# Later slots for the last normalising passes of the V slice, and a new order of work in the first group of a pre-normalised graph attention layer

## The chip, the cores and the metric

The kernel runs on one core of one Trainium2 chip, as a single launch. The metric is the device time of that launch in microseconds (us), from the start of the program to its end. A profiled execution also gives a span, from the first to the last recorded instruction.

## The reference

128 graphs of 128 nodes with 768 features each are normalised, rectified and sent through 12-headed attention (64 features a head) that is masked and biased by an adjacency matrix. All data are float32.

```
h = jnp.maximum(_layernorm(x, axis=-1), 0.0)
q, k, v = split(h @ Wq + bq), split(h @ Wk + bk), split(h @ Wv + bv)
scores = einsum('bhqd,bhkd->bhqk', q, k) / sqrt(64) + beta * adj
scores = where(adj > 0, scores, -9e15)
out = x + merge(softmax(scores) @ v)
```

## The kernel before, in words

**Groups and slices.** The 128 graphs are taken in 32 groups of four (G = 0 to 31). A group goes through three slices of matrix products: "qk0" (queries and keys of heads 0 to 5), "v" (all values) and "qk1" (queries and keys of heads 6 to 11). The scores, the softmax and the weighting of one group's heads are woven between the products of the slices that follow.

**Products.** A slice is a 3x3 block product. For groups 1 to 31 it is done with 15 block products (`PRODUCTS`) in place of 18. In qk0 and v each of them is done once more with seven small products on 128 columns (`product_z`, L482), for which the weights must first be turned into sums: `prepare` (L245) makes these once, during group 0, and stores them in DRAM (tensors `kept_qk` and `kept_v`). From there `load_T` (L292) brings them through a ring of five buffers (tag "T"), 448 KB for each product. The making of the sums uses the same ring of five, so a new sum waits until an older one has been stored.

Group 0 has no such sums yet. `plain_slice` (L761) gives it plain products: for each row half r (graphs 0-1, then graphs 2-3) and each output column block j it fills one PSUM bank with three steps k. Its matmuls are on L779. The q and k results are read out by ScalarE (L800), those of V by VectorE (L792).

**Slots.** A slot is one product (15 in a slice, `run`, L743), or one step k of `plain_slice` (18 in a slice). The dictionary `todo` lists what else is issued in a slot: after its matmuls and ahead of its read-out, or, with "post", behind the read-out. `then(at, f, ...)` enters it. From the V slice of group 0 on (`tc.manual_schedule()`, L978) each engine's queue follows the order of the code. Ahead of that line, so in qk0 of group 0, a planner with its own costs puts each engine's instructions in order, and `tc.issue_after(i)` is the means to force one instruction behind another on its engine.

**Openings.** The 15 products add up in four chains a, b, c, d of two PSUM banks each, and the bank's running sum is read out after each product. The first time that an output block is used, its tile is opened: ScalarE copies most of the banks (L509 and L511 for V, L514 to L517 for q and k) after VectorE has done a part of them (L508, L510). Later uses are VectorE additions (L521, L522). In `ZORDER` the products of slots 0, 1, 2, 3, 5 and 6 open a tile; those of slot 4 and of slots 7 to 14 only add. Slot 6 is product 5 of chain a, and the next product of chain a is product 10 in slot 8, which writes to the same banks.

**Normalising.** `norm` (L396) is four ScalarE passes for one graph (L400, in place on `x`). It needs the graph's rstd and shift. For groups 1 and 2 these come from `stats` (L316, VectorE), `moments_1` (L326: two small matmuls on L332, then VectorE) and `moments_2` (L342: matmuls on L346, VectorE, GpSimd); for group 0 in the same way for graphs 2-3 (`half`, L885) and by rows for graphs 0-1. `to_hT` (L402, VectorE, L406) then transposes a third of two graphs into a tile A00 to A12, where the first digit is the row half. Behind group 1 the V slice of group G normalises group G+1: graphs 0 and 1 in the posts of slots 0 to 3, graph 2 in slot 4 and graph 3 in slot 5 (L1040), and it transposes A01, A00, A02 and A11 in slots 5, 6, 7 and 9.

**Transfers.** All large transfers are issued by SyncE, in the order of its queue. `load_x` (L158) brings two graphs of x with four transfers into one of two buffers; `raw_qk` (L202) loads weight columns, eight transfers for the whole third slice (tile `wqk1`); `add_raw` (L922) loads a group's adjacency. A store of `kept_qk` or `kept_v` (L256) waits for GpSimd (L253, L254), which for most raw blocks waits for copies on ScalarE (L276).

Of the kernel before, what the change touches and what calls it, by code (L numbers as in the profile page):

```python
# [10 lines left out]
F32 = mybir.dt.float32  # L11
# [103 lines left out]
def direct(ctx, tc, x, adj, wq, bq, wk, bk, wv, bv, beta, out, bad):  # L115
# [645 lines left out]
    def plain_slice(G, sl, todo, rows=(0, 1)):  # L761

        n = 0
        for r in rows:
            for j in range(3):
                bank = take()
                p = bank.rearrange("p (i w) -> p i w", i=2)

                parts = (slice(0, N), slice(N, H2)) if sl == "qk0" and r == j == 0 else (slice(0, H2),)
                for at, k in [(at, k) for at in parts for k in range(3)]:  # L770
                    a, b = A[G, f"A{r}{k}"], wt[sl, f"B{k}{j}"]
                    for i in range(2):
                        for c in range(2):
                            lhs, rhs = b[:, c, i], a[:, c, at]
                            if sl == "v":
                                lhs, rhs = a[:, c, i * N:(i + 1) * N], b[:, c].rearrange("p i n -> p (i n)")
                            for q in range(0, P, HD) if sl == "qk1" else (slice(0, P),):
                                q = slice(q, q + HD) if sl == "qk1" else q
                                last = nc.tensor.matmul(p[q, i, at], lhs[:, q], rhs, start=(k == 0 and i == 0 and c == 0),  # L779
                                                        stop=(c == 1), skip_group_check=True)  # L780
                            turn()
# [188 lines left out]
    for r in range(2):  # L970
        then(5, load_x, 1, r)
    then(8, lambda: raw_qk(1, const.tile([P, NC * VH * 2], F32, name="wqk1"), ((0, 3),)))
    for n in range(5, 18):
# [7 lines left out]
    for g in range(GRP):  # L981
        then(2 * g, stats, 1, g)
        then(12 + g, norm, 1, g)
    then(8, lambda: mom.extend(moments_1(1, 0, GRP * NB)))
    then(10, lambda: moments_2(1, 0, GRP * NB, *mom))
    for n in range(18):
# [15 lines left out]
    for n in range(RING):  # L1002
        then(12 + n, load_T)
    then(13, add_raw, 1)
    plain_slice(0, "qk1", todo, (1, 0))

    for G in range(1, NG):
# [11 lines left out]
        if G == 1:  # L1019
            bias(1, 0, 2, 3, 5)  # L1020
            for r in range(2):
                then(r, load_x, 2, r)
            for g in range(GRP):
                then(5 + 2 * g, stats, 2, g)
            then(6, add_raw, 2)
# [9 lines left out]
        if more:  # L1035
# [3 lines left out]
            for g in range(2, GRP):  # L1039
                then(2 + g, norm, G + 1, g)  # L1040
            for name, at in (("A01", 5), ("A00", 6), ("A02", 7), ("A11", 9)):
                then(at, to_hT, G + 1, int(name[1]), int(name[2]))
# [177 lines left out]
```

## Time and profile before

| what | value |
|---|---|
| median of 3 runs | 2828.64 us (2823.12 to 2829.03) |
| the profiled execution | 2829.12 us |
| its span | 2827.0 us |
| TensorE matmuls busy | 2753.4 us, 97% of the span |
| granted TensorE clock, mean | 0.993 |

TensorE's own time is the first thing to look at, then what it waits for: the kernel's views list, for each engine, whom it waited for, how long in total, how often, and the longest wait. A timeline row gives start, duration, engine, line, operation, tiles and shape of merged instructions, and in brackets the idle time ahead of them and what ended it. A float32 matmul appears as two records. An engine's row in a window tells its busy time and count there, then the granted clock (PEclk), the busy share of the DMA engines and GB/s. Times that are given as places (such as "at 80.00") are us from the start of the span.

### The profile page before, as it was taken

The page shows a single profiled execution, that of the slowest core. Times are in us where ns is not written, and L with a number is a line of the kernel's source. Part 1 is how long each engine was busy: PE and PEld are TensorE (multiplying, and loading weights), DVE is VectorE, ACT ScalarE, POOL GpSimd, SP SyncE. Part 2 cuts the span into 40 slices and gives each one's busy share as a digit, 9 for nine tenths or more (in the row PEclk, how much of TensorE's full clock was granted, in tenths as well). Part 3 has the DMA queues.
Part 4 walks back from the last instruction along what each step waited for, and adds up shares of the span by engine and source line. Part 5 has one row for each costly group of instructions (what it writes and reads, how often), then busy time and mean ns, then how long its engine had stood idle before and what let it go on. Part 6 is the DMA issues. An engine that isn't in the chain of part 4 may idle for free.

```text
span 2827.0 us, 113416 instructions
## 1 busy us (share of the span) xinstructions
PE 2753.4 (97%) x46433; PEld 2391.0 (85%) x46433; DVE 2187.4 (77%) x4826; ACT 1357.7 (48%) x3999; POOL 2293.8 (81%) x4054
## 2 busy tenths in 40 slices
PE   8989999999999999999999999999999999999998
PEld 7678888888888888888888888888888888888887
DVE  3888777787777788787787787877777887877865
ACT  2345454555444554445553545554545544455533
POOL 2678988888888889888889888888888898888893
PEclk8999999999999999999999999999999999999999
DMA  9587778788778778778877788878787877788854
GB/s 220 188 253 223 235 225 248 253 244 236 230 225 260 250 237 234 229 233 260 249 231 233 227 244 257 246 231 234 222 260 250 235 236 231 231 259 249 234 182 130
DMA packets 526216, 660.87 MB, mean 234 GB/s; under 512 B 105460, under 2 KB 401664, under 8 KB 525696
## 3 DMA queue, kind: packets, MB, share of 16 engines
q1 hardware_dynamic: 525368, 653.20, 77.4%
q8 instruction: 368, 6.03, 0.9%
q14 instruction: 152, 1.25, 0.1%
q10 hardware_dynamic: 328, 0.40, 0.1%
HBM read 589.26 MB, written 64.21 MB: 231 GB/s over the span
## 4 chain that ended last, share of the span: by engine, by line


## 5 line engine op out<-in xcount | busy, mean ns | idle before, releaser
L630 ACT ACTIVATE o<-bank,sm 128x64 f32<-128x64 f32 x1524 | 355.0, 316 | 657.2 <-DVE sm L624 468.4
L495 PE MATMUL bank<-spbuf,T_qk 128*64 128x128 f32 x7440 | 658.7, 273 | 0.9 <-POOL qk L543 0.5
L495 PE MATMUL bank<-T_v,spbuf 128*64 128x128 f32 x7440 | 646.1, 273 | 0.1
L646 PEld LDWEIGHTS bank<-v,e 128*64 128x64 f32 x6048 | 412.3, 137 | 110.6 <-ACT o L630 0.2
L495 PEld LDWEIGHTS bank<-T_v,spbuf 128*64 128x64 f32 x7440 | 458.8, 137 | 0.4 <-ACT o L630 0.4
L495 PEld LDWEIGHTS bank<-spbuf,T_qk 128*64 128x64 f32 x7440 | 439.2, 137 | 1.4 <-POOL qk L543 0.8
L495 PE MATMUL bank<-T_v,S 128*64 128x128 f32 x4092 | 403.3, 274 | 36.0 <-ACT v L509 35.4
L646 PE MATMUL bank<-v,e 128*64 128x65 f32 x6048 | 433.8, 221 | 0.1
L581 ACT ACTIVATE qk<-bank,bqk 128x256 f32<-128x256 f32 x372 | 156.8, 475 | 550.8 <-PE bank L571 439.4
L495 PE MATMUL bank<-S,T_qk 128*64 128x128 f32 x4092 | 401.5, 274 | 4.2 <-DMA T_qk<-kept_qk 3.0
L571 PE MATMUL bank<-S,wqk 128*64 128x256 f32 x2976 | 389.2, 380 | 0.0
L613 DVE SCALAR_TENSOR_TENSOR e<-bank,biasT 128x512 f32<-128x512 f32 x378 | 240.5, 685 | 89.4 <-PE bank L609 89.3
L571 PE MATMUL bank<-S,qk_T 128*64 128x256 f32 x2480 | 305.3, 379 | 0.0
L495 PEld LDWEIGHTS bank<-T_v,S 128*64 128x64 f32 x4092 | 258.7, 137 | 49.4 <-ACT v L509 42.6
L521 DVE TENSOR_TENSOR v<-v,bank 128x512 f32<-128x512 f32 x310 | 211.8, 683 | 110.0 <-PE bank L495 96.6
L656 POOL TENSOR_TENSOR xo<-xo,o 128x512 f32<-128x512 f32 x189 | 242.0, 1280 | 58.9 <-ACT o L630 58.9
L551 POOL TENSOR_TENSOR v<-v 128x128 f32<-128x128 f32 x186 | 86.1, 463 | 223.6 <-ACT x L400 198.4
L521 DVE TENSOR_TENSOR qk<-qk,bank 128x512 f32<-128x512 f32 x310 | 210.7, 680 | 70.7 <-PE bank L495 34.8
L495 PEld LDWEIGHTS bank<-S,T_qk 128*64 128x64 f32 x4092 | 247.8, 137 | 14.8 <-issue 5.2
L587 DVE TENSOR_TENSOR qk<-qk,bank 128x512 f32<-128x512 f32 (+1 forms) x311 | 208.3, 670 | 43.4 <-PE bank L571 32.1
L616 ACT ACTIVATE e<-e 128x512 f32<-128x512 f32 x378 | 231.0, 632 | 21.8 <-DVE e L613 20.1
L418 POOL TENSOR_TENSOR spbuf<-S 128x128 f32<-128x128 f32 x341 | 182.9, 537 | 44.1 <-DVE S L411 44.1
(164 smaller groups left out, 5902.4 us busy)
## 6 DMA issues: line engine op xcount, KB each, us to landing
T_qk<-kept_qk SPq DMA_DIRECT2D x465, 448.0 KB, 5.0
T_v<-kept_v SPq DMA_DIRECT2D x465, 448.0 KB, 4.8
x<-in_x_dram SPq DMA_DIRECT2D x254, 192.0 KB, 4.7
xo<-in_x_dram SPq DMA_DIRECT2D x189, 256.0 KB, 5.1
out_dram<-xo SPq DMA_DIRECT2D x189, 256.0 KB, 5.0
half<-in_x_dram SPq DMA_DIRECT2D x232, 192.0 KB, 3.8
adj<-in_adj_dram SPq DMA_DIRECT2D x128, 64.0 KB, 2.5
kept_qk<-prep_qk SPq DMA_DIRECT2D x15, 448.0 KB, 3.9
```

The lines of the kernel that those rows point to most:

```text
L418: e.tensor_tensor(t[:, 0], a[:, 0, N:H2], a[:, 1, N:H2], ALU.add)
L495: nc.tensor.matmul(p[z // 4][q:q + HD, z % 4, :], lhs[:, q:q + HD], rhs, start=(first and z % 4 == 0), stop=True, skip_group_check=True)
L521: nc.vector.tensor_tensor(t[:, 0:4], t[:, 0:4], p[0], op)
L551: e.tensor_tensor(v[:, 0:2, 0:HD], heads(0), heads(3), ALU.add)
L571: nc.tensor.matmul(p[q:q + HD, i, :], lhs[:, q:q + HD], rhs, start=(first and i == 0 and c == 0), stop=(c == 1), skip_group_check=True)
L581: opened[0] = nc.scalar.activation(t[:, i, :], p[:, i, :], AF.Identity, bias=bqk[:, i, oc:oc + 1], scale=float(sign))
L587: added[G] = nc.vector.tensor_tensor(t[:, :, cols], t[:, :, cols], p[:, :, cols], ALU.add if sign > 0 else ALU.subtract)
L613: taken[0] = nc.vector.scalar_tensor_tensor(e, ps[oc, i].rearrange("p (g n) -> p g n", g=GRP), SCORE_CAP * ISCALE, biasT[G], op0=ALU.min, ...
L616: nc.scalar.activation(e, e, AF.Exp, scale=1.0 / ISCALE)
L630: nc.scalar.activation(o[:, b], pa[:, b, 0:HD], AF.Copy, scale=t[:, 1, b:b + 1])
L646: nc.tensor.matmul(pa[q:q + HD, 2 * g + i, :], es[G, oc, i][:, 2 * r + g, q:q + HD], vt[G, "v", r, h // 4][:, 4 * g + h % 4, :], start=Tru ...
L656: nc.gpsimd.tensor_add(t, t, o.rearrange("p a (b j) d -> p (a b) (j d)", j=2))
```

## The change

There are five edits.

1. In `plain_slice`, for the slice qk0 of group 0, every matmul of the second row half (graphs 2-3) is forced behind the last matmul of the first row half.
2. The loading of the third slice's weights (`raw_qk(1, ...)`, eight transfers) goes from slot 8 of that slice, in the planner's part, to slot 4 of the V slice of group 0, in the part that is ordered by the code.
3. In the V slice of group 0 the moments of group 1 go from slots 8 and 10 to 9 and 11, and its normalising passes from slots 12 to 15 to 13 to 16.
4. In the qk1 slice of group 0 the adjacency of group 1 is loaded in slot 11 and no longer in slot 13, and graphs 2-3 of group 2 in slot 16 (before: slot 1 of the next slice). Graphs 0-1 of group 2 go from slot 0 to slot 1 of that next slice, and its statistics take graphs 2, 3, 0, 1 in this order.
5. In the V slices of groups 1 to 30, the passes of graphs 2 and 3 of the next group go from slots 4 and 5 to slots 8 and 9, and the transpose A11 from slot 9 to slot 11.

```diff
     def plain_slice(G, sl, todo, rows=(0, 1)):
         n = 0
+        row0 = None
         for r in rows:
             for j in range(3):
+                row0 = last if (r, j) == (1, 0) and sl == "qk0" else row0
...
-                                last = nc.tensor.matmul(p[q, i, at], lhs[:, q], rhs, start=(k == 0 and i == 0 and c == 0),
-                                                        stop=(c == 1), skip_group_check=True)
+                                with ExitStack() as behind:
+                                    if sl == "qk0" and r == 1:
+                                        behind.enter_context(tc.issue_after(row0.ins))
+                                    last = nc.tensor.matmul(p[q, i, at], lhs[:, q], rhs, start=(k == 0 and i == 0 and c == 0),
+                                                            stop=(c == 1), skip_group_check=True)
...
-    then(8, lambda: raw_qk(1, const.tile([P, NC * VH * 2], F32, name="wqk1"), ((0, 3),)))
     for n in range(5, 18):
         then(n, after, step, 1 + n % 2)
     plain_slice(0, "qk0", todo)
...
     for g in range(GRP):
         then(2 * g, stats, 1, g)
-        then(12 + g, norm, 1, g)
-    then(8, lambda: mom.extend(moments_1(1, 0, GRP * NB)))
-    then(10, lambda: moments_2(1, 0, GRP * NB, *mom))
+        then(13 + g, norm, 1, g)
+    then(4, lambda: raw_qk(1, const.tile([P, NC * VH * 2], F32, name="wqk1"), ((0, 3),)))
+    then(9, lambda: mom.extend(moments_1(1, 0, GRP * NB)))
+    then(11, lambda: moments_2(1, 0, GRP * NB, *mom))
...
-    then(13, add_raw, 1)
+    then(11, add_raw, 1)
+    then(16, load_x, 2, 1)
     plain_slice(0, "qk1", todo, (1, 0))
...
-            for r in range(2):
-                then(r, load_x, 2, r)
+            then(1, load_x, 2, 0)
             for g in range(GRP):
-                then(5 + 2 * g, stats, 2, g)
+                then(5 + 2 * g, stats, 2, (g + 2) % GRP)
...
             for g in range(2, GRP):
-                then(2 + g, norm, G + 1, g)
-            for name, at in (("A01", 5), ("A00", 6), ("A02", 7), ("A11", 9)):
+                then(6 + g, norm, G + 1, g)
+            for name, at in (("A01", 5), ("A00", 6), ("A02", 7), ("A11", 11)):
                 then(at, to_hT, G + 1, int(name[1]), int(name[2]))
```

## The prediction

> **What bounds the kernel now.** I read the engines' busy times first, then the list of waits of TensorE (PE), then the timeline around each of its waits.
>
> ```profile
> PE 2753.4 (97%) x46433; PEld 2391.0 (85%) x46433; DVE 2187.4 (77%) x4826; ACT 1357.7 (48%) x3999; POOL 2293.8 (81%) x4054
> ```
> ```profile
> PE bank L495 <- ACT v L509: 35.4, 30, 1.2
> PE bank L779 <- DVE A L406: 6.9, 1, 6.9
> PE bank L332 <- DVE st L321: 6.7, 1, 6.7
> ```
>
> PE is busy 97% of the span, so a microsecond is only to be had where PE stands still or runs slowly. The list has one wait that comes back (30 times 1.2 us, for the opening copy L509 of V) and two long single ones. The first belongs to edit 5, the other two to edits 1 to 3, all in group 0. Here is one V slice, of group 4: ScalarE (ACT), PE, VectorE (DVE), then the slice's window.
>
> ```profile
> 449.91 4.49 ACT L400 ACTIVATE x<-x,block 128x192 f32<-128x192 f32 x10
> 454.30 0.47 ACT L509 ACTIVATE v<-bank 128x384 f32<-128x384 f32 x1
> ...
> 454.94 0.48 ACT L509 ACTIVATE v<-bank 128x384 f32<-128x384 f32 x1
> ...
> 468.16 0.47 ACT L581 ACTIVATE qk<-bank,bqk 128x256 f32<-128x256 f32 x1 [12.48 <-PE bank L571]
> ```
> ```profile
> 455.47 0.44 PE L495 MATMUL bank<-T_v,S 128*64 128x128 f32 x4 [1.18 <-ACT v L509]
> ```
> ```profile
> 452.80 0.29 DVE L510 TENSOR_TENSOR v<-bv_b,bank 128x128 f32<-128x128 f32 x1
> ...
> 457.81 0.70 DVE L406 STREAM_TRANSPOSE A<-x 128x512 f32<-128x512 f32 x1
> ```
> ```profile
> 440.00:468.00 28.00, 26.82 (x508) 24.97 (x505) 21.03 (x43) 14.83 (x35) 19.79 (x37) 1.00 0.85 273
> ```
>
> Ten passes in a row hold ACT from 449.91 to 454.40: two from the post of slot 3 and the eight of graphs 2 and 3. The openings of slots 5 and 6 stand behind them. The second copies its first bank out until 455.42, and PE, which wants that bank for product 10 in slot 8, starts at 455.47. The window's 28.00 less 26.82 is that same 1.18: PE has no other hole in this slice, and its clock stays at 1.00.
>
> **Edit 5, the V slices of groups 1 to 30.** No work is added or removed. Without the eight passes (8 x 0.45 = 3.6 us) ACT is free at about 450.9. DVE has finished its part of the second opening at 453.09 (L510), so ACT's two copies, 0.48 and about 0.4, end near 453.8. PE would start slot 8 at 455.47 - 1.18 = 454.29. So 0.5 us stay in hand, and the wait goes. The moved passes now run from 453.8 to 457.4, where ACT had nothing until 468.16; that 12.48 is their cover. A11 in slot 11 is issued two products later than at 457.81, so it finds graph 3 ready. DVE, next in line, had done slot 7's sum before PE came to slot 9. I see no other wait that comes in its place, except in group 1:
>
> ```profile
> 203.87 0.44 PE L495 MATMUL bank<-T_v,A 128*64 128x128 f32 x4 [2.48 <-DVE v L521]
> ```
>
> There DVE, loaded with weight sums and masks, holds PE later in the same slice, and PE would only arrive 1.18 us earlier at that wait. So the term is 29 x 1.18 = **34.2 us** (35.4 if group 1 gains too).
>
> **Edit 1, the order in qk0 of group 0.** PE's timeline there:
>
> ```profile
> 20.39 0.29 PE L332 MATMUL bank<-st,mean 128*64 128x16 f32 x4
> 21.66 0.29 PE L346 MATMUL bank<-dev,mean 128*64 128x16 f32 x4 [0.97 <-DVE dev L339]
> 28.85 28.89 PE L779 MATMUL bank<-A,spbuf 128*128 128x256 f32 x120 [6.90 <-DVE A L406]
> 57.58 10.52 PE L779 MATMUL bank<-spbuf,A 128*128 128x256 f32 x48
> ...
> 80.00 0.43 PE L332 MATMUL bank<-st,mean 128*64 128x32 f32 x4 [6.71 <-DVE st L321]
> 80.36 6.29 PE L779 MATMUL bank<-spbuf,A 128*128 128x256 f32 x16
> ```
> ```profile
> 28.00:34.00 6.00, 5.15 (x12) 4.17 (x13) 5.92 (x12) 0.64 (x4) 2.28 (x3) 0.50 1.03 203
> ```
> ```profile
> 80.00:85.00 5.00, 5.00 (x15) 4.04 (x16) 4.79 (x14) 1.40 (x6) 2.33 (x3) 0.50 0.57 223
> ```
>
> At 20.68 PE has only one of six banks done, and it then waits until 28.85 for the transposes of graphs 2-3. At full clock a record takes 10.52 / 48 = 0.219 us. The 120 records behind the wait should take 26.3 and took 28.89: 2.6 us lost to the clock of 0.50. With the edit, the two other banks of graphs 0-1 (48 records, 10.5 us) come first, if their weights are there:
>
> ```profile
> 12.57 2.93 SPq L197 DMA_DIRECT2D spbuf<-in_L_gnn_Wk_dram  x4
> ```
> ```profile
> DMA to landing us min/median/max: 7.0/7.2/7.3
> ```
> ```profile
> 24.44 3.61 ACT L400 ACTIVATE x<-x,shift,rstd 128x192 f32<-128x192 f32 x8 [3.04 <-POOL shift L355]
> ```
> ```profile
> 28.08 1.90 DVE L406 STREAM_TRANSPOSE A<-x 128x512 f32<-128x512 f32 x3 [5.70 <-ACT x L400]
> ```
>
> The last of these loads (the second line is their time to landing) is issued at 15.2 and lands at about 22.4. Until then PE has four records (0.9 us) that need only Wq. The other 116 take 25.4 us, the moments 0.3: the slice ends near 48.1, where before it was 28.85 + 28.89 = 57.7. That is **9.6 us**. The passes (24.44) and transposes (done at 29.98) are ready before PE wants them at 33. Bounds: 0, if the read-outs that ACT now gets earlier were queued ahead of those passes; 0.97 + 6.90 + 2.6 = 10.5.
>
> **Edits 2 and 3, the moments of group 1.** PE waits at 80.00 for the last statistics on DVE. What made DVE late:
>
> ```profile
> 61.86 0.29 DVE L251 TENSOR_TENSOR prep_qk<-spbuf 128x128 f32<-128x128 f32 x1 [12.25 <-DMA kept_qk<-prep_qk]
> ...
> 65.59 1.54 DVE L227 TENSOR_TENSOR prep_qk<-prep_qk,spbuf 128x512 f32<-128x512 f32 x2
> ...
> 75.05 1.13 DVE L321 BATCH_NORM_STATS2 st<-x 128x6 f32<-128x192 f32 x4
> ...
> 78.72 1.12 DVE L321 BATCH_NORM_STATS2 st<-x 128x6 f32<-128x192 f32 x4
> ...
> 87.70 0.28 DVE L251 TENSOR_TENSOR prep_v<-spbuf 128x128 f32<-128x128 f32 x1
> ```
> ```profile
> 58.51 1.29 ACT L276 COPY prep_qk<-spbuf 128x128 f32<-128x128 f32 x6
> ```
> ```profile
> 45.59 3.76 SPq L197 DMA_DIRECT2D wqk<-in_L_gnn_Wk_dram  x4
> 50.58 28.23 SPq L256 DMA_DIRECT2D kept_qk<-prep_qk  x13
> ```
> ```profile
> DMA to landing us min/median/max: 10.4/10.9/11.2
> ```
>
> DVE stood 12.25 us for a ring buffer. The stores that free it were issued from 50.58 on, behind the weights of the third slice, and took 10.4 to 11.2 us to land (last line: the first three of them). Next come the copies at 58.51, queued on ACT behind the last read-out of qk0. Edit 2 takes the weights away from there; edit 1 brings that read-out 9.6 us forward. From the end of the last product (57.7) to the sum at 65.59 were 7.9 us, with a slow store in it; from 65.59 to the end of the statistics (79.84) 14.25 us of nearly closed work. Shifted by 9.6, the statistics end at 70.2; with a store that lands 2 us sooner, at 68. I take 69. PE, with its moments behind ten steps now (8 x 0.219 = 1.75 each), gets there at 48.1 + 17.5 = 65.6 and waits 3.4. Against 6.71 that is 3.3 us; the clock took 6.29 - 16 x 0.219 = 2.8 us more behind 80.36, of which I count half: **4.7 us** together. Bounds: 0, and 6.71 + 2.8 = 9.5.
>
> What is queued behind the moved weights: SP's next stores, so the ring, so DVE from slot 10 on. The statistics of slot 4 are at 75.05 and slot 10's first step that needs a later store at 87.70; shifted like the rest, by 10.8, that is 64.3 and 76.9. Eight loads started at 65 or 66 keep the next store from landing until about 77 (11 to 12 us, as above), so DVE would meet it about in time. Nearest cover: PE's scores at 102.71 are read out by DVE from 106.15, and until then PE has spare banks.
>
> ```profile
> 102.71 2.85 PE L609 MATMUL bank<-qk 64*64 64x128 f32 x96
> ```
> ```profile
> 106.15 3.67 DVE L613 SCALAR_TENSOR_TENSOR e<-bank,biasT 128x512 f32<-128x512 f32 x6
> ```
>
> I take 0 and keep 0 to 12 us of loss (one whole landing) for the range. The weights themselves land at 77, ahead of the qk1 slice near 84.
>
> **Edit 4, the loads around group 1's first slice.**
>
> ```profile
> 154.37 0.70 PE L495 MATMUL bank<-S,T_qk 128*64 128x128 f32 x4 [2.98 <-DMA T_qk<-kept_qk]
> ```
> ```profile
> 154.00:158.00 4.00, 3.63 (x44) 3.63 (x46) 1.12 (x2) 0.00 (x0) 3.41 (x8) 0.59 1.07 381
> ```
> ```profile
> 141.14 3.09 SPq L163 DMA_DIRECT2D x<-in_x_dram  x4
> ```
>
> Four x loads (3.09 us of issue) sat between two loads of prepared weights; they now go before the slice. I take **3 us** of the wait (2.98) and its clock (4 x 0.41 = 1.6); bounds 0 and 4.6.
>
> [...]
>
> **Sum.** 34.2 + 9.6 + 4.7 + 3 = 51.5 us. The profiled execution took 2829.1 (span 2827.0 and 2.1 around it, 0.5 above the median of the runs): 2829.1 - 51.5 = **2777.6 us**.
>
> **Rivals.** (A) The first group gives its gain back: the store behind the moved weights holds DVE, and PE waits for it later instead (up to 12 us), or the planner's other choices leave edit 1 empty. For it: DVE is closely packed from 61.86 to 106.15. Against: spare banks. Then 34.2 and 0 to 8 remain, about 2791. (B) Edit 5 doesn't do what it says: the wait in slot 8 stays and another engine ends it, since DVE's share of the same opening ends only at 453.09. Then only the first group's 17.3: 2812. Against: the 0.5 us in hand. (C) Slower: A11 in slot 11 reaches DVE with less of the slice left to catch up, so that PE waits as it does at 203.87, 2.48 per group. It decides if DVE runs over 1.2 us behind PE at slot 13; the price is 29 x (2.48 - 1.18) = 38 against 17 gained: 2850. Against: two slots before that, A11 cost 0.70 at 457.81 without a wait.
>
> **Chances.** Forecast (2768 to 2786) 0.62, A (2786 to 2797) 0.24, B 0.07, C 0.05, and A with B, near nothing, 0.02. The lower end takes all upper bounds: 35.4 + 10.5 + 9.5 + 4.6 = 60, 2769. With A the range is 2768 to 2797. About 0.2% is what a measurement of this kernel can tell from no change. Faster 0.93, same 0.02, slower 0.05.
>
> **What would show it.** Edit 5: the row of 30 waits for L509 gone from PE's list, V slices 1.2 us shorter, L400 right behind the openings. Edit 1: no wait for L406, the v products starting near 48. Edits 2 and 3: a wait for L321 of 2 to 5 us near 69, and no 12-us wait of DVE before it; a new wait of DVE for kept_qk near 77. Edit 4: no wait near slot 7 of group 1. The prediction is wrong if PE's list has a new entry 29 times.

## The result, and the profile after

| what | before | after |
|---|---|---|
| median | 2827.44 us (2823.12 to 2829.03, 4 runs) | 2780.26 us (2777.87 to 2781.26, 4 runs) |
| the profiled execution | 2829.12 us | 2781.26 us |
| its span | 2827.0 us | 2779.2 us |
| granted TensorE clock, mean | 0.993 | 0.996 |

The ratio is 0.9834 (0.9817 to 0.9851): 47.2 us or 1.7% faster. The forecast was 2777.6, in a range of 2768 to 2797. As a gain it was 51.5 us, counted from the profiled execution (2829.1). The total is close to the forecast, but in part because two terms missed in opposite directions. From L784 on, the line numbers of the changed kernel are those of before plus 5.

First TensorE's busy time, and the list of whom it waited for (total us, times, longest):

```profile
PE 2744.4 (99%) x46433; PEld 2401.3 (86%) x46433; DVE 2187.9 (79%) x4826; ACT 1363.2 (49%) x3999; POOL 2297.7 (83%) x4054
```
```profile
PE bank L784 <- DMA spbuf<-in_L_gnn_Wk_dram: 4.7, 2, 3.2
PE bank L495 <- DVE v L521: 4.1, 3, 3.5
PE bank L332 <- DVE st L321: 3.8, 2, 3.4
PE bank L609 <- POOL qk L542: 3.0, 1, 3.0
PE bank L784 <- DVE v L797: 2.5, 1, 2.5
...
PE bank L495 <- ACT v L509: 0.5, 2, 0.3
```

The wait for L509 that came back 30 times is gone (0.5 us are left of 35.4), and so is the wait for the transposes L406. The rest are single waits. Four of these rows are longer than before (2.3 for the loads `spbuf`, 3.5 for L521, 1.2 for GpSimd) or new (L797), all in groups 0 and 1.

**The steady groups.** The same V slice as before (that of group 4, now about 12 us earlier), its window and ScalarE's rows:

```profile
440.00:468.00 28.00, 28.00 (x404) 23.23 (x402) 20.57 (x40) 10.59 (x28) 24.34 (x48) 1.00 0.80 261
```
```profile
440.80 0.49 ACT L509 ACTIVATE v<-bank 128x384 f32<-128x384 f32 x1 [0.22 <-DVE v L508]
...
441.45 3.62 ACT L400 ACTIVATE x<-x,block 128x192 f32<-128x192 f32 x8
454.73 0.84 ACT L581 ACTIVATE qk<-bank,bqk 128x256 f32<-128x256 f32 x2 [9.67 <-PE bank L571]
```

TensorE is busy for all 28.00 us. The eight passes (L400) now run behind the last opening, and 9.67 us of idle time still follow them. To see what a group gained, take the first product of the qk1 slice in two groups that follow each other, before and after:

```profile
294.78 1.03 PE L571 MATMUL bank<-S,qk_T 128*64 128x256 f32 x8
...
380.50 1.03 PE L571 MATMUL bank<-S,qk_T 128*64 128x256 f32 x8
```
```profile
284.17 1.03 PE L571 MATMUL bank<-S,qk_T 128*64 128x256 f32 x8
...
368.48 1.03 PE L571 MATMUL bank<-S,qk_T 128*64 128x256 f32 x8
```

Before, a group lasted 380.50 - 294.78 = 85.72 us; now it lasts 368.48 - 284.17 = 84.31. That is 1.41 us less, where the forecast had the 1.18 that the list of waits showed.

**The first two groups.** TensorE's timeline in group 0:

```profile
24.35 25.95 PE L784 MATMUL bank<-A,spbuf 128*128 128x256 f32 x112 [3.21 <-DMA spbuf<-in_L_gnn_Wk_dram]
50.14 10.52 PE L784 MATMUL bank<-spbuf,A 128*128 128x256 f32 x48
...
71.01 0.31 PE L332 MATMUL bank<-st,mean 128*64 128x32 f32 x4 [3.44 <-DVE st L321]
...
87.38 3.67 PE L784 MATMUL bank<-A,wqk 128*64 128x256 f32 x32
...
98.23 2.39 PE L784 MATMUL bank<-A,wqk 128*64 128x256 f32 x14 [2.52 <-DVE v L797]
```

The second slice starts at 50.14 (forecast 48.1, before 57.58), and the moments wait 3.44 us (forecast 3.4). Then comes a wait that was not there before, 2.52 at 98.23. VectorE's timeline shows what lies behind it, and the store's own row in the view of line L256 gives its time from issue to landing:

```profile
84.91 0.29 DVE L251 TENSOR_TENSOR prep_v<-spbuf 128x128 f32<-128x128 f32 x1 [6.97 <-DMA kept_qk<-prep_qk]
```
```profile
68.47 2.32 SPq L197 DMA_DIRECT2D wqk<-in_L_gnn_Wq_dram  x4
70.83 1.99 SPq L197 DMA_DIRECT2D wqk<-in_L_gnn_Wk_dram  x4
73.66 0.34 SPq L256 DMA_DIRECT2D kept_qk<-prep_qk  x1
```
```profile
DMA to landing us min/median/max: 11.2/11.2/11.2
```

The eight moved weight loads are issued from 68.47 on. The next store, at 73.66, lands 11.2 us later, and VectorE stands 6.97 us for the ring buffer that it frees. From there VectorE is late. It stands 2.34 us more for a store of `kept_v` (until 94.25), and its read-out of V and its weight sums come late, and through these GpSimd and the scores of group 1. Two more waits of TensorE follow in group 1's V slice, and beside them stands the row of a kernel (e1, below) that has edit 5 alone, and so no late store:

```profile
170.98 2.37 PE L609 MATMUL bank<-qk 64*64 64x128 f32 x32 [2.98 <-POOL qk L542]
...
195.46 0.69 PE L495 MATMUL bank<-T_v,A 128*64 128x128 f32 x4 [3.48 <-DVE v L521]
```
```profile
201.48 0.44 PE L495 MATMUL bank<-T_v,A 128*64 128x128 f32 x4 [3.47 <-DVE v L521]
```

So the second of these waits does not come from the late store. It was 2.48 before (in e2, without edit 5, it is 2.48 too), and it is 3.46 to 3.49 in every kernel with edit 5 whose sums in this slice are unchanged: TensorE, spared the stop in slot 8, arrives there earlier and waits longer.

And these waits cost clock too. The windows behind the waits of 2.52, 2.98 and 3.48 us (the figure behind POOL's instructions is the granted clock):

```profile
98.00:103.00 5.00, 4.77 (x30) 2.84 (x32) 4.88 (x9) 0.31 (x1) 3.12 (x4) 0.66 0.70 274
171.00:176.00 5.00, 4.90 (x80) 3.99 (x84) 2.56 (x5) 4.02 (x10) 4.76 (x6) 0.68 0.03 8
195.00:200.00 5.00, 4.54 (x58) 4.54 (x60) 4.97 (x10) 0.00 (x0) 3.47 (x8) 0.69 0.13 25
```

Each window loses 5 x (1 - 0.66 to 0.69) = 1.6 to 1.7 us, and so does the one behind the wait of 3.44 (0.66 from 71 to 76). To follow the lead through the first two groups, here are the first products of the slices qk0, v and qk1 of group 1, before and then after:

```profile
135.96 0.39 PE L495 MATMUL bank<-S,T_qk 128*64 128x128 f32 x4
...
172.68 0.42 PE L495 MATMUL bank<-T_v,S 128*64 128x128 f32 x4
...
209.06 0.60 PE L571 MATMUL bank<-S,qk_T 128*64 128x256 f32 x4
```
```profile
128.66 0.39 PE L495 MATMUL bank<-S,T_qk 128*64 128x128 f32 x4
...
161.10 0.42 PE L495 MATMUL bank<-T_v,S 128*64 128x128 f32 x4
...
199.86 0.60 PE L571 MATMUL bank<-S,qk_T 128*64 128x256 f32 x4
```

The qk1 slice of group 0 began at 99.10 before and begins at 87.38 now, a lead of 11.72 us. It falls to 7.30 by group 1's qk0 (the late store: 2.52 and its clock), grows to 11.58, and falls to 9.20 (the waits of 2.98 and 3.48). So 9.2 us come from groups 0 and 1. The spans differ by 2827.0 - 2779.2 = 47.8, which leaves 38.6 for the 29 V slices and the end. The places agree: from the qk1 slice of group 1 to that of group 31 it was 2782.99 - 209.06 = 2573.9 us, and now it is 2735.09 - 199.86 = 2535.2, which is 38.7 less.

The fall to 7.30 was not a lasting loss. Three experiments below (e2, e5, e7) have the same code up to TensorE's wait for V's read-out. Here are their profiles beside that of the changed kernel, as places where a slice begins, and e2's row for that wait:

| profile | VectorE's waits for `kept_qk`, `kept_v` | TensorE's wait for L797 | qk1, group 0 | qk0, group 1 | v, group 1 |
|---|---|---|---|---|---|
| changed kernel | 6.97, 2.34 | 2.52 | 87.38 | 128.66 | 161.10 |
| e5 | 6.94, 2.41 | 2.81 | 85.08 | 126.55 | 158.97 |
| e2 | 6.56, 0.74 | 0.26 | 87.43 | 125.06 | 162.14 |
| e7 | 6.41, 1.15 | 0.73 | 86.16 | 124.26 | 161.28 |

```profile
96.02 16.27 PE L784 MATMUL bank<-A,wqk 128*64 128x256 f32 x146 [0.26 <-DVE v L797]
```

VectorE's long wait is there each time. TensorE's wait follows the second, shorter one, which differs between executions. The changed kernel and e2 begin the qk1 slice of group 0 at the same place. e2 hardly waits and begins group 1 3.6 us earlier, and yet its V slice begins 1.0 us later: in the slice between, which takes 37 us in e2 and e7 and 32.4 in the other two, TensorE waits more when it comes early. What sets the place where that V slice begins stays open.

### The profile page after: what moved, and what is told of

Read it like the earlier page. It is cut to its first block, busy times and chain, and to the rows that moved or that the text cites. A ratio compares the mean times of both kernels' runs of the same rounds, so it can differ in the third digit from the quotient of the medians.

```text
span 2779.2 us, 113442 instructions
## 1 busy us (share of the span) xinstructions
PE 2744.4 (99%) x46433; PEld 2401.3 (86%) x46433; DVE 2187.9 (79%) x4826; ACT 1363.2 (49%) x3999; POOL 2297.7 (83%) x4054
## 4 chain that ended last, share of the span: by engine, by line
## 5 line engine op out<-in xcount | busy, mean ns | idle before, releaser
L646 PEld LDWEIGHTS bank<-v,e 128*64 128x64 f32 x6048 | 419.3, 137 | 106.0 <-issue 0.8
L551 POOL TENSOR_TENSOR v<-v 128x128 f32<-128x128 f32 x186 | 97.9, 526 | 224.5 <-DVE v L521 224.5
L521 DVE TENSOR_TENSOR v<-v,bank 128x512 f32<-128x512 f32 x310 | 211.7, 683 | 70.2 <-PE bank L495 60.5
L521 DVE TENSOR_TENSOR qk<-qk,bank 128x512 f32<-128x512 f32 x310 | 210.5, 679 | 68.0 <-PE bank L495 32.7
L571 PEld LDWEIGHTS bank<-S,qk_T 128*64 128x64 f32 x2480 | 167.9, 137 | 58.9 <-issue 0.2
```

What stands on the lines that cost most here:

```text
L521: nc.vector.tensor_tensor(t[:, 0:4], t[:, 0:4], p[0], op)
L551: e.tensor_tensor(v[:, 0:2, 0:HD], heads(0), heads(3), ALU.add)
L571: nc.tensor.matmul(p[q:q + HD, i, :], lhs[:, q:q + HD], rhs, start=(first and i == 0 and c == 0), stop=(c == 1), skip_group_check=True)
L646: nc.tensor.matmul(pa[q:q + HD, 2 * g + i, :], es[G, oc, i][:, 2 * r + g, q:q + HD], vt[G, "v", r, h // 4][:, 4 * g + h % 4, :], start=Tru ...
```

## The experiments

All twelve were timed in five rounds beside the kernel before, in three sets (kernel before 2827.34, 2828.87 and 2827.38). "Gain" is the time of before in that set less the kernel's own. Against the changed kernel's 47.2, gains that differ by under about 3 us can hardly be told apart: the intervals of the ratios are about 0.15% to each side.

| kernel | median us | ratio to before | gain us |
|---|---|---|---|
| changed kernel | 2780.26 | 0.9834 (0.9817 to 0.9851) | 47.2 |
| e1: edit 5 alone | 2787.97 | 0.9861 (0.9845 to 0.9876) | 39.4 |
| e2: edits 1 to 4 alone | 2818.92 | 0.9971 (0.9959 to 0.9982) | 8.4 |
| e3: weights from ScalarE at once | 2777.52 | 0.9823 (0.9809 to 0.9836) | 49.8 |
| e4: edit 2 undone | 2786.00 | 0.9854 (0.9839 to 0.9870) | 41.3 |
| e5: half a dose of edit 5 | 2792.79 | 0.9877 (0.9862 to 0.9892) | 36.1 |
| e6: edit 1 undone | 2783.60 | 0.9842 (0.9828 to 0.9855) | 43.8 |
| e7: edit 4 undone | 2779.89 | 0.9833 (0.9819 to 0.9846) | 49.0 |
| e8: weights in three parts | 2777.09 | 0.9821 (0.9808 to 0.9835) | 51.8 |
| e9: weights gated on ScalarE | 2778.87 | 0.9825 (0.9812 to 0.9838) | 50.0 |
| e11: e8, moments two slots later | 2775.67 | 0.9813 (0.9800 to 0.9826) | 51.7 |
| e12: e8, weight sums spread | 2774.85 | 0.9815 (0.9801 to 0.9828) | 52.5 |
| e13: all three | 2773.82 | 0.9806 (0.9792 to 0.9819) | 53.6 |

My theory after the result had two parts. The steady groups gain 1.41 us each, because the shown idle time understates a stop. The first group gives half of its gain back through the store behind the moved weights. The rivals: part of edit 5's surplus comes from the first groups, and the first group's loss has nothing to do with the place of the weights.

### The two halves: e1 and e2

e1 is the kernel before with edit 5 alone:

```diff
-                then(2 + g, norm, G + 1, g)
-            for name, at in (("A01", 5), ("A00", 6), ("A02", 7), ("A11", 9)):
+                then(6 + g, norm, G + 1, g)
+            for name, at in (("A01", 5), ("A00", 6), ("A02", 7), ("A11", 11)):
```

> The kernel before with edit 5 alone (passes of graphs 2 and 3 in slots 8 and 9, A11 in slot 11). If a wait is worth the idle time that the list of waits shows, 29 x 1.18 = 34 us are gained: about 2793. If it is worth the longer distance between two starts of PE (a group lasted 85.72 us before and 84.31 after the change, 1.41 less), 29 x 1.41 = 41, less what group 1 gives back: 2786 to 2789, and the idle time in the V slice is 0 while a group is 1.41 shorter. If the passes only change places with another wait: 2820 or more.

e2 is the changed kernel with these lines put back.

> The changed kernel without edit 5, so edits 1 to 4 alone. By the traces the first groups gave 9.2 us up to the qk1 slice of group 1, where the prediction had 17.3: about 2818 by the traces, 2810 by the prediction. If the two halves of the change help each other through PE's earlier arrival, it comes out below 2815 together with edit 5 alone above 2789.

They gained 39.4 and 8.4 us, together 47.8 against 47.2. So the two halves add up within the noise, and edit 5 alone is worth 39.4 us. That is 1.36 for each of 29 groups. The lower end of its interval (1 - 0.9876 = 1.24%, 35.1 us) lies just above the 34.2 of the forecast. In e1's profile the way from group 1's qk1 slice to group 31's is 2741.35 - 205.63 = 2535.7 us, 38.2 less than before. So the rival that the surplus comes from the first groups can explain about 1 us of it. The first group's edits bring 8.4 us (5 to 12 by the interval) and not 17.3.

### A dose of edit 5: e5

```diff
-                then(6 + g, norm, G + 1, g)
+                if g == 2:
+                    then(4, norm, G + 1, g)
+                else:
+                    then(5, norm, G + 1, g, 0, 2)
+                    then(9, norm, G + 1, g, 2, 4)
```

> Dose of edit 5: the last two normalising passes of graph 3 stay behind slot 9, as in the changed kernel, and the six before them (graph 2, and the first half of graph 3) go back to slots 4 and 5. If the gain of edit 5 is the openings that TensorE is spared, and if it is counted from start to start of its products, part of the stop comes back, 0.2 to 0.9 us in each of 29 groups: a steady group of 84.5 to 85.2 us instead of 84.31, and a total of 2786 to 2805. If the shown idle time of 1.18 us is the whole of it and half the passes make half the stop, 29 x 0.59 = 17 us, 2797. If any two passes behind slot 5 make the whole stop, the time goes to 2819, that of the run without edit 5; if the first six passes had no part in it, it stays at 2780.

2792.79 us. TensorE's list of waits, then the first qk1 product of two groups in a row:

```profile
PE bank L495 <- ACT v L509: 9.4, 30, 0.3
```
```profile
282.30 1.25 PE L571 MATMUL bank<-S,qk_T 128*64 128x256 f32 x10
...
367.16 1.25 PE L571 MATMUL bank<-S,qk_T 128*64 128x256 f32 x10
```

The wait is back 30 times with 0.31 each. Two passes of 0.45 us moved away take 0.9 from 1.18, which leaves 0.28. So each of the last two passes ahead of the opening delays TensorE by its own length. The first ones cost it nothing: eight passes are 3.6 us of ScalarE, and the stop is 1.41. The group lasts 84.86 us, 0.55 longer than after, for a shown wait of 0.31. With 1.41 for 1.18 that makes two points: about 0.23 us more than shown, each time. The rows of before ahead of the wait at 455.47 say where that comes from:

```profile
453.68 0.39 PE L495 MATMUL bank<-T_v,S 128*64 128x128 f32 x4
453.89 0.39 PE L495 MATMUL bank<-T_v,spbuf 128*64 128x128 f32 x4
```

These groups of matmuls start every 0.21 to 0.22 us, yet each is drawn 0.39 long: they overlap. The next one was due at 453.89 + 0.22 = 454.11 and started at 455.47. It came 1.36 us late, where the idle time, counted from the drawn end of the last record, is 1.18. "Half the passes, half the stop" (2797) and the all-or-nothing cases (2819, 2780) are out.

### The place of the weights: e4, e3, e8, e9

e4 undoes edit 2 alone: the weights are issued in slot 8 of the first slice again.

```diff
+    then(8, lambda: raw_qk(1, const.tile([P, NC * VH * 2], F32, name="wqk1"), ((0, 3),)))
...
-    then(4, lambda: raw_qk(1, const.tile([P, NC * VH * 2], F32, name="wqk1"), ((0, 3),)))
```

> The changed kernel with edit 2 undone: the third slice's weights are loaded from the planner's part again, ahead of most stores. If those loads made VectorE late, its wait for the ring of some 10 us before the V slice is back, the wait for the moments grows from 3.4 to 6 or more, and the wait of 6.97 us in slot 10 is gone. If edit 2 is worth what the prediction counted, 3 to 5 us slower than the changed kernel (2783 to 2785); if it only moves the loss from the moments to slot 10, within 2 us of it.

2786.00: 5.7 us slower than the changed kernel, 1 us more than the expected 2783 to 2785, with intervals that just overlap. Its rows on TensorE and VectorE:

```profile
49.58 10.52 PE L784 MATMUL bank<-spbuf,A 128*128 128x256 f32 x48
...
80.94 0.43 PE L332 MATMUL bank<-st,mean 128*64 128x32 f32 x4 [13.93 <-DVE st L321]
```
```profile
62.80 0.29 DVE L251 TENSOR_TENSOR prep_qk<-spbuf 128x128 f32<-128x128 f32 x1 [12.03 <-DMA kept_qk<-prep_qk]
```

This is the clearest view of the study. Edit 1 is there, and the second slice starts at 49.58, 8 us sooner than before. Yet VectorE is released at 62.80 (before 61.86), and the moments run at 80.94 (before 80.00). TensorE merely waits 13.93 us in place of 6.71. What held VectorE were the stores behind the weights, and not the read-outs that edit 1 brings forward. So up to the moments the gain is edit 2's, and edit 1 has a share only once edit 2 is made.

e3 issues the weights from ScalarE in place of SyncE, forced behind ScalarE's last copy for the weight sums (`raw_qk` gets the engine as a parameter, not shown):

```diff
-                    nc.scalar.copy(t[:, z], b[:, c, i])
+                    copied[0] = nc.scalar.copy(t[:, z], b[:, c, i])
...
-    then(4, lambda: raw_qk(1, const.tile([P, NC * VH * 2], F32, name="wqk1"), ((0, 3),)))
+    def weights():
+        with tc.issue_after(copied[0].ins):
+            raw_qk(1, const.tile([P, NC * VH * 2], F32, name="wqk1"), ((0, 3),), nc.scalar)
+
+    then(4, weights)
```

> The changed kernel with the third slice's weights issued from ScalarE's queue, behind its copies for the prepared sums (near 53 us), in place of SyncE's queue. Theory of the order in the queue: the store of the sums no longer stands behind eight loads, so VectorE's wait of 6.97 us in slot 10 falls under 2, PE's wait of 2.52 us for V's bank and its time at half clock go, and the wait of 2.98 us for GpSimd in group 1 shrinks: 5 to 8 us less than the changed kernel, 2772 to 2775. Rival, the bandwidth: the 2.36 MB take the same DMA engines from the stores whichever queue they come from, VectorE waits as long but earlier, and the time stays within 1.5 us of the changed kernel.

2777.52, between the two theories. ScalarE issued them from 51.55 on (the last at about 75) and not from 68. VectorE's 6.97 and TensorE's 2.52 were gone. But the stores of that earlier time were slowed instead: the six issued between 52 and 62 took 4.8 to 6.2 us to land, where those of the changed kernel took 2.5 to 2.7. VectorE waited 1.88 and 2.39 us for them, and the moments wait grew:

```profile
74.62 0.43 PE L332 MATMUL bank<-st,mean 128*64 128x32 f32 x4 [7.77 <-DVE st L321]
```

So the loss isn't only a matter of the queue: here the stores beside the weights took 4.8 to 6.2 us, though the weights came from another queue. In these runs it is a matter of when the weights move.

e8 stays on SyncE, with the weights in three parts:

```diff
-    then(4, lambda: raw_qk(1, const.tile([P, NC * VH * 2], F32, name="wqk1"), ((0, 3),)))
+    w1 = const.tile([P, NC * VH * 2], F32, name="wqk1")
+    for at, part in ((4, (0, 1)), (9, (1, 2)), (14, (2, 3))):
+        then(at, lambda part=part: raw_qk(1, w1, (part,)))
```

> The third slice's weights are issued in three parts, in slots 4, 9 and 14 of the second slice, all from SyncE as in the changed kernel. Theory (the late store of T10 lies behind the weights in SyncE's queue): only a third of them lies ahead of it, VectorE's wait of 6.97 us near 85 falls to 0 to 3 us, TensorE's wait for the biased values and the half clock behind it go, the moments wait stays near 3.4 us; 3 to 5 us less than the changed kernel, 2775 to 2777. Rival: the transfers are slow because of their bytes on all the queues, wherever they stand; then the last part lands late, the third slice itself waits for weights, and the time is the same or up to 5 us longer.

2777.09, 3.2 us less than the changed kernel (4.6 by the gains, which take each set's own time of before). That fits the theory, but the intervals overlap, so the time alone does not show it. The wait at 98.23 is gone, and VectorE's longest wait behind the weights is 3.15:

```profile
83.99 0.69 DVE L227 TENSOR_TENSOR prep_v<-spbuf,v_B 128x512 f32<-128x512 f32 x1 [3.15 <-DMA kept_v<-prep_v]
```
```profile
69.49 0.31 PE L332 MATMUL bank<-st,mean 128*64 128x32 f32 x4 [3.14 <-DVE st L321]
...
92.25 7.99 PE L784 MATMUL bank<-A,wqk 128*64 128x256 f32 x72
```

e9 issues the weights whole from ScalarE, but behind a small copy that needs the statistics of slot 4:

```diff
+    def weights():
+        nc.scalar.copy(tables, st[1][:, 2 * NB, 0:1])
+        raw_qk(1, const.tile([P, NC * VH * 2], F32, name="wqk1"), ((0, 3),), nc.scalar)
+
-    then(4, lambda: raw_qk(1, const.tile([P, NC * VH * 2], F32, name="wqk1"), ((0, 3),)))
+    then(4, weights)
```

> The third slice's weights go out from ScalarE's queue, behind one small copy there that waits for the statistics of slot 4 of the second slice, so that they are neither ahead of a store on SyncE nor beside the stores that the statistics wait for. Theory: the moments wait stays near 3.4 us, VectorE's wait of 6.97 us near 85 is gone, so are TensorE's 2.52 us behind it and the half clock, and GpSimd starts group 1's weight sums earlier (its 2.98 us shrink): 4 to 7 us less than the changed kernel, 2773 to 2776. Rival: the time lost in the first group is a matter of all bytes together; then the wait only moves (to the moments as with the weights on ScalarE at once, or to the third slice's start), and the time is 2777 to 2781.

2778.87, where 2773 to 2776 was expected. The mechanism did act: the moments wait was 3.45, TensorE's 2.52 was gone, VectorE's longest wait here was 4.05, and group 1's qk1 slice began at 195.57, as in e8 (195.41) and 4.3 us sooner than after. The time did not follow by as much. In the steady part of e9's profile some groups last 84.8 to 85.6 us in place of 84.31, with waits for prepared weights (`T_v`, `T_qk`) of up to 0.88. Single groups of that length also occur without the gate (85.33 in e8, 85.38 in e13), so nothing here ties them to it.

### Edits 1 and 4 alone: e6 and e7

e6 takes out the order of edit 1:

```diff
-                                    if sl == "qk0" and r == 1:
+                                    if False:
```

> The changed kernel with edit 1 alone undone: the products of graphs 0 and 1 are queued as before, so that one of graphs 2 and 3 stands ahead of them on TensorE. Theory (the order starts the second slice about 7 us sooner, and 3.4 us of that are given back at the moments, with the half clock behind): the second slice starts 6 to 8 us later than in the changed kernel, the moments wait of 3.44 us goes, the late store keeps its place, and the time is 2 to 5 us more: 2782 to 2785. Rival 1 (nothing else moved, as the prediction summed it): the statistics are late by as much, the moments wait stays, and the time is 7 to 10 us more: 2787 to 2790. Rival 2 (VectorE's date, set by its stores, bounds the first group, and TensorE's start does not matter): within 1.5 us of 2780.

2783.60: 3.3 us more by the medians, 2.3 by the ratios (0.9842 against 0.9834), with intervals that overlap. Its profiled run, 2790.47, was the slowest of five, so only places are read from it:

```profile
55.40 10.52 PE L784 MATMUL bank<-spbuf,A 128*128 128x256 f32 x48
...
75.07 0.31 PE L332 MATMUL bank<-st,mean 128*64 128x32 f32 x4 [2.24 <-DVE st L321]
```

The second slice starts 5.3 us later than after and the moments come 4.1 us later. So with edit 2 in place VectorE does follow TensorE, and edit 1 is worth some 2 to 3 us by the time, within the 2 to 5 of the first theory but not clear of the noise. Not all of that theory held: a moments wait of 2.24 stayed, and the wait for V's read-out grew to 4.86 in this profile. The first rival (7 to 10) falls. The second (no effect) falls by the places, though not clearly by the time.

e7 puts edit 4 back:

```diff
-    then(11, add_raw, 1)
-    then(16, load_x, 2, 1)
+    then(13, add_raw, 1)
...
-            then(1, load_x, 2, 0)
+            for r in range(2):
+                then(r, load_x, 2, r)
...
-                then(5 + 2 * g, stats, 2, (g + 2) % GRP)
+                then(5 + 2 * g, stats, 2, g)
```

> The changed kernel with edit 4 undone (the x rows of group 2 in slots 0 and 1 of group 1 again, the added matrices of group 1 in slot 13 of group 0). Theory: the 2.98-us wait of before and the half clock behind it come back in group 1, and its first slice grows by 3 to 4.3 us: 2783 to 2785. Rival: group 1's first slice is shorter because the work of the first group ended in another order, not through edit 4; then it stays within 1 us of the changed kernel.

2779.89, the same as the changed kernel. The wait of 2.98 for a load of prepared weights, which edit 4 was to remove, does not come back. The longest wait of TensorE in that slice is another:

```profile
132.30 1.12 PE L495 MATMUL bank<-spbuf,T_qk 128*64 128x128 f32 x8 [2.54 <-POOL spbuf L419]
```

In e1, which has neither edit 4 nor the others of the first group, the wait for these loads is there (2.04 at 152.99). So it belongs to the first group's old timing, and the edits ahead of it had removed it already. One thing came as the theory said: the first slice of group 1 grew, from 32.44 us to 37.02 (161.28 - 124.26). But in e2, which has edit 4, it takes 37.08, and in e7 too the slice only began earlier and ended where it ended in the changed kernel (161.28 and 161.10). By this edit 4 is worth 0, with some 2 us of uncertainty.

### What is left in groups 0 and 1: e11, e12, e13

Each starts from e8. e11 moves the moments two slots on:

```diff
-        then(13 + g, norm, 1, g)
+        then(14 + g, norm, 1, g)
...
-    then(9, lambda: mom.extend(moments_1(1, 0, GRP * NB)))
-    then(11, lambda: moments_2(1, 0, GRP * NB, *mom))
+    then(11, lambda: mom.extend(moments_1(1, 0, GRP * NB)))
+    then(13, lambda: moments_2(1, 0, GRP * NB, *mom))
```

> As e8_weights_split, with the moments of the second group two slots later in the second slice (slots 11 and 13, their normalising passes from slot 14 on). Theory (the statistics end at about 69.5, whatever TensorE does, and two slots are 3.5 us of products): the wait of 3.14 us and the half clock behind it (about 1.7 us) go, 3 to 5 us less than with the split alone: 2772 to 2774. Rival: the normalising passes and the transposes behind them are late by as much, TensorE waits in the third slice in place of the second, and the time stays at 2776 to 2778.

e12 spreads the weight sums of group 1's V slice:

```diff
-                for at, n in enumerate((3, 4, 5, 6, 7, 8, 9, 10, 13, 14)):
-                    then(at + 3, sum_weights, "qk1", n)
+                for at, n in enumerate((3, 4, 5, 6, 7)):
+                    then(2 * at + 3, sum_weights, "qk1", n)
...
+        if G == 1:
+            for at, n in enumerate((8, 9, 10, 13, 14)):
+                then(at + 1, sum_weights, "qk1", n)
```

> As e8_weights_split, with five of the ten weight sums that lie in the V slice of group 1 moved into the next slice and the other five spread over it. Theory: VectorE has too much work in that V slice, the 3.49-us wait of TensorE for its moved T tile there goes, and so does part of the half clock behind it: 3 to 5 us less than with the split alone, 2772 to 2774. Rival: the next slice has no room for the sums either and TensorE waits there: no gain, 2776 to 2779.

e13 has both.

> The three together: weights split, moments two slots later, weight sums spread. If the two waits (3.14 and 3.49 us) and their half clocks are independent, the gains add: 6 to 10 us less than with the split alone, 2767 to 2771. If the earlier start only makes another part late, as the earlier edits of the first group did, half of it or less is left: 2772 to 2776.

2775.67, 2774.85 and 2773.82, against 2777.09 for e8: 1.4, 2.2 and 3.3 us less, where 3 to 5, 3 to 5 and 6 to 10 were expected (for e13 with the alternative of half or less, 2772 to 2776, which came true). By the ratios, which allow for each set's own time of before, 0.8, 0.6 and 1.5 thousandths; each interval overlaps with e8's. In e11 the moments wait shrank to 1.83, but the second pair of small matmuls now waited too, for VectorE, which does the moments' arithmetic in its turn behind the sums:

```profile
77.66 0.31 PE L346 MATMUL bank<-dev,mean 128*64 128x32 f32 x4 [2.59 <-DVE dev L339]
```

In e12 the wait in group 1's V slice is 2.88 in place of 3.49. So e11 mostly moved its wait, and e12 shortened one by a sixth. e13 is the fastest kernel of the study. It is 6.4 us below the changed kernel by the medians, with intervals (0.9792 to 0.9819, and 0.9817 to 0.9851) that barely overlap.

## Why the prediction was right, and where not

**Sum.** Right by sign, by size (2.7 us off as a time, 4.3 as a gain, since the forecast counted from 2829.1 and the median of before is 2827.4) and by its main mechanism. But it was 51.5 = 34.2 + 17.3, and it became 47.2 = 39.4 + 8.4 (e1, e2), within 0.6. The two errors, 5.2 too little and 8.9 too much, hid each other in part, and that is luck: with 34.2 for edit 5 the time would have been 2784.8, close to the 2786 where rival A's range begins. By the places, the lead of 17.3 that was forecast for group 1's V slice was 11.6: 2.6 were missing at the qk1 slice of group 0, and the 3 of edit 4 behind it. Another 2.4 went in that V slice.

**Edit 5, 34.2.** The mechanism was right at each step: the row of L509 gone, the passes behind the openings, their cover still 9.67 us, no new entry 29 times. Rivals B and C did not occur. The figures of the prediction (453.09 + 0.48 + 0.4) put the end of the copies at 454.0 and not 453.8, so 0.3 us were in hand by them, not 0.5; that was still enough. To leave group 1 out of the count was right: there the wait for L521 grew from 2.48 to 3.48 instead. The mis-sized term is the stop itself: 1.41 us (85.72 - 84.31) in place of 1.18. The prediction read the idle time of overlapping records as the loss. 29 x 1.41 = 40.9 is an upper bound, since some groups now last 84.4 to 85.4, and TensorE meets short waits for prepared weights (`T_v`: 1.5 us in 4 waits). The places give 38.7 (38.2 in e1), the medians of e1 39.4.

**Edit 1, 9.6.** The second slice started 57.58 - 50.14 = 7.4 us sooner. The step that fell short is the landing of the first slice's last weights: TensorE got them at 24.35 and not at 22.4, after a wait of 3.21 (issued at 15.2 as before, the last one took 8.9 us to land, and not the 7.0 to 7.3 read from the profile of before), and part of the slice then ran slowly (112 records in 25.95 us against 112 x 0.219 = 24.5). The larger error is to have counted edit 1 as a term by itself. e4 shows that without edit 2 its lead is lost whole at the moments, and e6 that with it some 2 to 3 us remain.

**Edits 2 and 3, 4.7, with the weights' own cost at 0.** The wait for the moments, 3.44, is the forecast's 3.4. But all came 2 us later, at 71.01 and not 69, and the clock behind it cost 1.7 where 1.4 was allowed. The 12-us wait of VectorE is gone, as said. The step that failed is "DVE would meet it about in time". The prediction counted the 11 to 12 us of a landing from the start of the eight loads. In the rows of before, 10.4 to 11.2 us run from the store's own issue, which came 8.75 us (50.58 - 41.83) behind that of the first load. Now the loads were issued from 68.47 and not at 65 or 66, the store at 73.66, and it landed at 84.9 and not at 77, while VectorE wanted its buffer at 77.9. The price lay inside the stated bound of 12: 6.97 us of VectorE, of which TensorE felt 2.52 and 1.7 of clock in this profile, but only 0.26 in e2's. The cover that I named, spare banks until the scores are read out, held for only part of it: the V read-outs L797 stand in the same queue of VectorE. This is the mechanism of rival A. The 4.4 us that it took here (11.72 to 7.30) were back by group 1's V slice (11.58). There 2.4 us were lost, and of the two waits behind that loss, the 2.98 for GpSimd fits VectorE's delay (it is 0.86 in e2 and e7, where VectorE's second wait was short), and the 3.48 belongs to edit 5, as said. The 8.4 us of e2 lie just above the 0 to 8 that rival A leaves the first group; its 2791 was not reached, because edit 5 was worth more. Edit 3 was not tried alone.

**Edit 4, 3.** The trace seemed to confirm it: the wait is gone, and group 1's first slice lasts 32.44 us (161.10 - 128.66) in place of 36.72. e7 and e2 show that this was no effect of edit 4: the wait is gone without the edit, and with it the slice can last 37.08. In the profile above the slice was only catching up on what had been lost ahead of it. The step that failed: that a wait seen in the profile of before would still be there once three other edits had changed the timing ahead of it.

**The clock.** The 1.4 us allowed for the clock behind the moments, half of the 2.8 behind 80.36 before, was an estimate of mine, and no run shows that half. The trace shows a clock of 0.66 over the 5 us behind the wait of 3.44, so 1.7 us, and 0.66 also behind the shorter wait of 2.52. The last section has more of these waits.

## What to carry to other kernels

Measure a repeated stop from start to start, by comparing the distance of like records with and without it; the idle time that a list shows can be too small when records overlap (1.18 shown, 1.41 gained). Before adding up edits in a start-up phase, find the one engine whose date ends the phase (here, up to the moments, VectorE behind its stores), since a lead on another engine is then worth nothing by itself (in e4, 8 us of lead on TensorE, and the moments at 80.94 in place of 80.00). A wait that one profile shows in such a phase is not yet a loss: compare the places a slice or two later, and in more than one execution. And a bulk load that is moved is issued ahead of something else: name the next store behind it, count its landing from its own issue (11.2 us here), and try to split the load if that store has a reader that waits (in e8 the wait went, though the gain in time is not clear of the noise).

## What the runs showed of the hardware that I had not expected

Half clock came behind some short waits and not behind some longer ones: behind 2.52 in the changed kernel (0.66 over the 5 us from 98.00) and behind 1.83 in e11 (0.62 over the 4.5 us from 69.50), but not behind 2.24 in e6 (1.00 over the 4 us from 75.00), and not behind 3.48 in e5 (1.00 up to 195.04, in its rows below). In these runs the length of a wait alone does not decide. Between 7 and 2775 us of the changed kernel's trace the granted clock falls to 0.50 at 24.06, 71.84, 99.15, 170.83 and 194.72, and each time it is back at 1.00 3.41 us later. These falls lie 47.78, 27.31, 71.68 and 23.89 us apart, which is 14, 8, 21 and 7 times 3.41 to within 0.1 us. Here is the stretch of 3.41 us with most of the wait of 3.44 and the one behind it, then two such stretches of e5 that share the wait of 3.48 (ended at 193.29):

```profile
68.43:71.84 3.41, 0.83 (x7) 0.77 (x8) 3.38 (x11) 0.00 (x0) 1.87 (x4) 1.00 1.03 306
71.84:75.26 3.42, 3.42 (x10) 2.67 (x9) 3.31 (x9) 0.00 (x0) 2.28 (x4) 0.50 1.10 207
```
```profile
188.21:191.62 3.41, 1.61 (x28) 1.37 (x26) 3.41 (x6) 0.63 (x1) 3.31 (x6) 1.00 0.85 266
191.62:195.04 3.42, 1.75 (x28) 1.51 (x28) 3.39 (x7) 0.00 (x0) 2.82 (x5) 1.00 0.32 113
```

In the first pair TensorE is idle for 2.58 of 3.41 us, and the next stretch runs at 0.50. In the second it is idle for 1.80 and 1.67, and the clock is 1.00 in both. That the idle time within one such stretch decides, and not the whole wait, is my estimate from these four rows. In the row from 71.84 TensorE is busy throughout at 0.50, which costs 3.42 x 0.5 = 1.7 us. So the wait of 2.52 cost about 4.2 us in the changed kernel (5 x 0.34 = 1.7 of it as clock), and the wait of 3.48 in e5 nothing beyond itself up to 195.04. Behind a longer wait more was lost: in e7, behind 4.50, 16 records took 6.17 us from 69.26 on, where 16 x 0.219 is 3.5, so 2.7 us (the clock was 0.79 over the 10 us from 70.00).

The start of the program differs from one execution to the next. The last weights of the first slice kept TensorE waiting 3.21 us in the changed kernel's profile and 0.67 in e8's. In e5's it did not wait there at all, with the same code up to that point, and the second slice started at 46.30 in place of 50.14:

```profile
46.30 10.52 PE L784 MATMUL bank<-spbuf,A 128*128 128x256 f32 x48
...
68.84 0.43 PE L332 MATMUL bank<-st,mean 128*64 128x32 f32 x4 [5.11 <-DVE st L321]
```

Of that head start of 3.8 us, 2.2 were left at the moments (68.84 against 71.01). So places in the first groups carry some 2 us of chance when two profiles are compared, which is why the table of medians, and not the traces, decides on edits 1 and 4, and decides on edit 1 only within its noise.
